# Two-layer graph attention on one core: x and x1 loaded as permuted blocks and transposed on VectorE instead of TensorE

## The chip, the core and the metric

The kernel runs on one core of one Trainium2 chip. A core has five engines that follow their own instruction streams and wait for each other on semaphores: TensorE (matrix products, PE in the profile; its weight loads are PEld), VectorE (DVE), ScalarE (ACT), GpSimd (POOL) and SyncE (SP), which here issues all DMAs. The metric is the device time of one execution in microseconds (us).

## What is computed

The input `x` holds 128 graphs of 64 nodes with 768 features. The first layer is graph attention with 12 heads of 64 features and a gate; the second is masked attention with 6 heads of 128 features. Each layer's result is added to its input and normalized.

```python
# layer 0, per graph
h = einsum('bnd,ade->bane', x, W); th = tanh(h)
attn = th @ w_src + swapaxes(th @ w_dst)          # per head, node by node
attn = softmax(where(adj, leaky(attn), -999))
feat = elu(attn @ h + b)
gate = sigmoid(x @ H_w.T + H_b)
x1 = layernorm(x + gate * feat + (1 - gate) * x)
# layer 1, per graph
q, k, v = x1 @ Wq, x1 @ Wk, x1 @ Wv               # plus biases
out = layernorm(x1 + softmax(mask(q @ k.T / sqrt(128), adj)) @ v @ Wf + bf)
```

## The kernel before

Two graphs make a tile of 128 tokens on the 128 partitions; two tiles make a pair; there are 32 pairs (`NP`). Phase A (to about 1590 us of the profile) runs layer 0 for every pair and the product of layer 1 that gives `v`; phase B runs the rest of layer 1. Only phase A's code changes, apart from the row order in which phase B's weights are loaded.

The large products multiply a pair's two tiles by 768x768 weights with a seven-product scheme for 2x2 blocks. One such product is seven blocks (`Product.matmuls(i)`, i = 0 to 6), each of three matmuls of 128x128 by 128x384; the profile records each matmul twice, so a block is six records (x6) of L203. Blocks read the transposed tiles `T` (blocks 0, 1 and 5) and four sums of parts of them, `S` (blocks 2, 3, 4 and 6), which GpSimd makes in `token_sums` (L252 to L255). After each block, `evict` takes the accumulator out of PSUM: ScalarE copies a `snap` (L381) after blocks 0, 2 and 3, VectorE adds after blocks 1, 4 and 5 (L404 or L423), ScalarE copies after block 6. Block 4 waits for the `snap` of block 2, and block 6 for VectorE's eviction of block 4. Three products run for a pair: h (`start_h`), the gate (`start_g`), and later, on x1, v (`start_v`).

A matmul contracts over partitions, so a tile has to be transposed before it is multiplied. `transposed` (L368) does this on TensorE: six transposes of 128x128 into two PSUM tiles (L375), each copied to SBUF by ScalarE (L376). `chunk0` takes every third column of a half, so that the contraction index runs as (half, partition, c); `chunk1` takes 128 columns in a row. x is transposed with `chunk0`, x1 with `chunk1`, and the rows of the weights are loaded to match.

Nothing is scheduled by a planner. `at(step, f)` files each piece of work under a step; `run` executes the steps in order, and within a step in the order of filing, which goes by pair. This fixes the order of the instructions on every engine, and the order of the DMAs on SP. Pair `p` starts at step `o = 21 p`. In its frame: h blocks at 0 to 6, gate blocks at 7 to 13, v blocks at 56 to 62, so that in a steady window of 21 steps one pair's h and gate blocks are followed by the v blocks of an earlier pair. Around them:

- x of the pair is loaded at -20 (`load`, L314), transposed at -6 and -5, summed at -4.
- For each tile (`Tile0`; tile 1 with s = o, tile 0 with s = o + 5): tanh at s + 6 or 7; the two products with `w_src` and `w_dst` on GpSimd (L444, L451) and their sums on VectorE (L448, L454) at 7 to 9; a small transposition (L456), an exchange through DRAM (`dst_out`, `dst_in`, L462 and L470) and an exchange of halves (`exchange`, L480); adding (L492 on GpSimd, L495 on ScalarE) at 17; mask, maximum, subtraction and exp (L499 to L507) at 18 and 19; sum, reciprocal (L511, L513) and GpSimd's scaling (L514) at 20; the probabilities are transposed on TensorE (L525, L530) at 23 and multiplied by h (L543) at 24; then VectorE's `elu` (L562) and ScalarE's `e` (L569), VectorE's mixes (L573, L574, L582, L583) at 26 and 27, the statistics (L278 to L289) and GpSimd's rstd and shift (L290 to L293) at 28, ScalarE's normalization (L297) at 29, and the store of x1 to DRAM (`spill`, L592) at 30.
- x1 is transposed at 42 and 43 from its SBUF tile and stored transposed for phase B (L663), and summed at 44.

Tiles come from pools with fixed numbers of buffers; an instruction that writes a buffer waits until the last reader of its previous use is done.

Of the kernel before, what the change touches and what calls it, by code (L numbers as in the profile page):

```python
# [9 lines left out]
F32 = mybir.dt.float32  # L10
# [5 lines left out]
P = 128  # L16
# [45 lines left out]
def kernel(  # L62
# [31 lines left out]
    nc = tc.nc  # L94
    NB, S, D = x.shape
# [3 lines left out]
    NC = D // P  # L99
    HALF = D // 2  # L100
    CH = NC // 2
    NT = NB * S // P
    NP = NT // 2
    assert S == 64 and DH == P and E == 64 and HALF == 384 and A == 12

    x_t = x.rearrange("(t g) n d -> t (g n) d", g=2)
# [11 lines left out]
    ident = const.tile([P, P], F32, name="ident")  # L118
# [32 lines left out]
    def load15(wb, src, k):  # L151

        kb, c = divmod(k, 2)
        nc.sync.dma_start(
            wb[:, 3 * kb : 3 * kb + 3, c, :],
            src[k * P : (k + 1) * P, :].rearrange("p (n o) -> p n o", n=3),
        )

    def weight15_sum(wb, k, eng):
        to, a, b, sign = WEIGHT_SUMS[k]  # L160
        eng.tensor_tensor(wb[:, to], wb[:, a], wb[:, b], SIGN[sign])
# [7 lines left out]
    def weight_plain(wb, src, blocks):  # L169
        for kh, oh in blocks:  # L170
                nc.sync.dma_start(
                    wb[:, SLOT[kh, oh]],
                    src[kh * HALF : (kh + 1) * HALF, oh * HALF : (oh + 1) * HALF].rearrange(
                        "(c p) o -> p c o", p=P
                    ),
                )

# [71 lines left out]
    def token_sums(Ss, Ta, Tb):  # L249

        tt = nc.gpsimd.tensor_tensor
        tt(Ss[:, 0], Tb[:, :CH], Tb[:, CH:], ALU.add)  # L252
        tt(Ss[:, 1], Ss[:, 0], Ta[:, :CH], ALU.subtract)
        tt(Ss[:, 2], Ta[:, :CH], Tb[:, :CH], ALU.subtract)
        tt(Ss[:, 3], Ta[:, CH:], Ss[:, 1], ALU.subtract)  # L255
# [14 lines left out]
    x1_d = [spill.tile([P, D], F32, name=f"x1_d{t}") for t in range(NT)]  # L270
    v_d = [spill.tile([P, D], F32, name=f"v_d{t}") for t in range(NT)]
    xT_d = [spill.tile([P, 2, NC, P], F32, name=f"xT_d{p}") for p in range(NP)]
# [27 lines left out]
    def phase_a(ctx):  # L300
        k6 = ctx.enter_context(tc.tile_pool(name="k6", bufs=2))
        k3 = ctx.enter_context(tc.tile_pool(name="k3", bufs=1))
        k1 = ctx.enter_context(tc.tile_pool(name="k1", bufs=1))
        small = ctx.enter_context(tc.tile_pool(name="small", bufs=3))
        psa = ctx.enter_context(tc.tile_pool(name="psa", bufs=4, space=bass.MemoryType.PSUM))

        st = [dict() for _ in range(NP)]
# [6 lines left out]
        def load(p):  # L314
            d = st[p]
            d["x"] = []
            for i in range(2):
                t = xb[:, (2 * p + i) % 7]
                nc.sync.dma_start(t, x_t[2 * p + i])
                d["x"].append(t)  # L320
            d["adj"] = small.tile([P, 2, S], U8, name="adj")
            nc.sync.dma_start(d["adj"], adj_p[p])
# [18 lines left out]

        def load_hrow(oc):

            name = ("gt", "gt", "gt", "z", "e", "th")[oc]
            hrows[oc] = k3.tile([P, D], F32, name=name, bufs=3 if oc < 3 else 1)
            nc.sync.dma_start(hrows[oc], H_w[oc * P : (oc + 1) * P, :])

# [14 lines left out]
        def chunk0(src, k):  # L362
            return src.rearrange("p (h q c) -> p h c q", h=2, c=CH)[:, k // CH, k % CH, :]

        def chunk1(src, k):
            return src[:, k * P : (k + 1) * P]

        def transposed(src, chunk):  # L368

            dst = k3.tile([P, NC, P], F32, name="T", bufs=4)  # L370
            for half in range(2):
                ps = psa.tile([P, CH, P], F32, name="pa")
                for c in range(CH):
                    k = half * CH + c
                    nc.tensor.transpose(ps[:, c, :], chunk(src, k), ident)  # L375
                nc.scalar.copy(dst[:, half * CH : (half + 1) * CH, :], ps)  # L376
            return dst

# [5 lines left out]
        def sums(d):  # L384
            Ss = k6.tile([P, 4, CH, P], F32, name="S")
            token_sums(Ss, *d["T"])
            d["S"] = Ss
# [20 lines left out]
        def start_h(d):  # L408
            d["h"] = [k3.tile([P, D], F32, name="h", bufs=3) for _ in range(2)]
            d["W"] = product(d, lambda i, c: w0_v[:, i, :, c, :], into(d["h"]))  # L410

        def start_g(d):
            d["g"] = [k3.tile([P, D], F32, name="gt", bufs=3) for _ in range(2)]
            d["G"] = product(d, lambda i, c: w1[:, i, c, :], into(d["g"]))

        def start_v(d):
            def sink(k, ps, kept):
                i, half = PLACE[k]
                o = k1.tile([P, HALF], F32, name="v", bufs=3)
                if kept is None:  # L420
                    nc.scalar.copy(o, ps)
                else:
                    nc.vector.tensor_tensor(o, ps, kept, ALU.add)  # L423
                nc.sync.dma_start(v_d[2 * d["p"] + i][:, halves(half)], o)

            d["V"] = product(d, lambda i, c: w2[:, i, c, :], sink)
# [5 lines left out]
        class Tile0:  # L432
# [124 lines left out]
            def elu(self):  # L557

                self.z = k3.tile([P, D], F32, name="z")
                zv = self.z.rearrange("p (j h e) -> p j h e", h=2, e=E)  # L560
                for h2 in range(2):
                    nc.vector.tensor_tensor(  # L562
                        zv[:, :, h2, :],
                        self.pos[h2],
                        b_bc[:, None, :].to_broadcast([P, A // 2, E]),
                        ALU.add,
                    )
                self.e = k3.tile([P, D], F32, name="e")
                nc.scalar.activation(self.e, self.z, AF.Exp, bias=neg_one)  # L569

            def mix1(self):
# [26 lines left out]
        def at(step, *fs):  # L598
            events.setdefault(max(step, 0), []).extend(fs)

        def dense(d, key, i):
            d[key].matmuls(i)
            d[key].evict(i)
# [17 lines left out]
        for p in range(NP):  # L621
            d, o = st[p], N * p
            d["p"] = p
            if p:
                at(max(o - 20, 1), lambda p=p: load(p))

            def xT(d, i):
                d.setdefault("T", []).append(transposed(d["x"][i], chunk0))

            at(o - 6, lambda d=d: xT(d, 0))  # L630
            at(o - 5, lambda d=d: xT(d, 1))
            at(o - 4, lambda d=d: sums(d))
            at(o, lambda d=d: start_h(d))
            at(o + 7, lambda d=d: start_g(d))
            for i in range(7):
                at(o + i, lambda d=d, i=i: dense(d, "W", i))
                at(o + 7 + i, lambda d=d, i=i: dense(d, "G", i))
            for i, s in ((1, o), (0, o + 5)):
                t = Tile0(p, i)
                at(s + 6 + (i == 0), t.tanh, t.cap)  # L640
                at(s + 7, t.src_mul)
                at(s + 8, t.src_sum, t.dst_mul)
                at(s + 9, t.dst_sum, t.dst_out, t.exchange)
                at(s + 13, t.dst_in)
                at(s + 14, t.gate)
                at(s + 17, t.add)
                at(s + 18, t.mask)
                at(s + 19, t.top)
                at(s + 20, t.total)
                at(s + 23, t.probs)  # L650
                at(s + 24, t.aggregate)
                at(s + 25, t.elu)
                at(s + 26, t.mix1)
                at(s + 27, t.mix2)
                at(s + 28, t.norm1)
                at(s + 29, t.norm2)
                at(s + 30, t.spill)

            def x1T(d, i):
                if i == 0:  # L660
                    d["T"] = []
                d["T"].append(transposed(d["x"][i], chunk1))
                nc.sync.dma_start(xT_d[d["p"]][:, i], d["T"][i])  # L663

            at(o + 42, lambda d=d: x1T(d, 0))
            at(o + 43, lambda d=d: x1T(d, 1))

            def reload_T(d):
                d["T"] = []
                for i in range(2):  # L670
                    t = k3.tile([P, NC, P], F32, name="T", bufs=4)
                    nc.sync.dma_start(t, xT_d[d["p"]][:, i])
                    d["T"].append(t)

            if p != NP - 4:
                at(o + 44, lambda d=d: sums(d))

            v = o + {NP - 4: 84, NP - 2: 50, NP - 1: 45}.get(p, 56)
            if p == NP - 4:
                at(v - 7, lambda d=d: reload_T(d))  # L680
                at(v - 3, lambda d=d: sums(d))
            at(v, lambda d=d: start_v(d))
            for i in range(7):
                at(v + i, lambda d=d, i=i: dense(d, "V", i))
# [5 lines left out]
        o = N * (NP - 1)  # L690
# [410 lines left out]
```

## Time and profile before

| | |
|---|---|
| runs (3) | median 3029.0 us, 3027.24 to 3031.79 |
| profiled execution | 3025.7 us, span 3023.9 us |
| TensorE clock granted | 0.993 |
| one pair, steady (start of x's first L375 transposes, 622.25 to 669.72) | 47.47 us |
| TensorE busy, 200 to 1400 us | 199.0 to 199.2 of every 200 us |
| VectorE, ScalarE, GpSimd busy, 600 to 800 us | 132.2, 82.5, 117.3 of 200 us |
| DMA queue of SP | 223,808 packets, 257.16 MB, 25.7% of 16 engines' span |

The profile page gives busy times and groups of instructions. A group is one line of the code on one engine, with count, total and mean duration, and the idle time of the engine just before it, with what ended it. The chain of waits goes back from the last instruction, at each step to what released it. A timeline lists instructions with their start, duration and the idle time before them. Line numbers are those of the kernel before; the sum of the busy times of overlapping matmuls is not their duration.

### The profile page before, as it was taken

What the parts mean: (1) busy time and instruction counts of PE and PEld (TensorE: products, weight loads), DVE (VectorE), ACT (ScalarE), POOL (GpSimd) and SP (SyncE); (2) the same over time, 40 slices, a digit from 0 to 9 for tenths busy, and PEclk for the clock granted to TensorE, in tenths of its full rate; (3) what the DMA queues carried; (4) which work ended last, traced back from release to release, by engine and by line L of the source; (5) the groups of instructions that cost most, each with busy time, mean ns of one, the idle gap of its engine ahead of it and who ended that gap; (6) DMA issues with size and microseconds to landing.
All of it is one profiled execution on the core that took longest, in us unless ns stands there. A gap on an engine that the chain in (4) does not pass through costs nothing.

```text
span 3023.9 us, 49367 instructions
## 1 busy us (share of the span) xinstructions
PE 2935.8 (97%) x18852; PEld 2139.9 (71%) x18852; DVE 1798.6 (59%) x3531; ACT 937.8 (31%) x1743; POOL 1640.8 (54%) x1648
## 2 busy tenths in 40 slices
PE   7899999999999999999899999999999999999997
PEld 4566666666666666666557888888888888888886
DVE  4666666666676666766674555555555555555556
ACT  3343443434434444444422122222112222211221
POOL 3756565665656556565574444554544455454445
PEclk9999999999999999999999999999999999999999
DMA  5232232222322222232252121222112122211221
GB/s 158 67 98 92 89 110 77 98 87 93 105 82 98 82 98 98 84 103 82 87 173 80 49 85 60 78 85 82 57 63 85 59 80 85 81 57 64 85 79 69
DMA packets 224044, 260.31 MB, mean 86 GB/s; under 512 B 91713, under 2 KB 169281, under 8 KB 223809
## 3 DMA queue, kind: packets, MB, share of 16 engines
q1 hardware_dynamic: 223808, 257.16, 25.7%
q8 instruction: 150, 2.46, 0.3%
q14 instruction: 86, 0.70, 0.1%
HBM read 143.43 MB, written 101.06 MB: 81 GB/s over the span
## 4 chain that ended last, share of the span: by engine, by line
PE 66%; POOL 16%; DVE 12%; ACT 2%; issue 2%; DMA 1%; SPq 0%; DVEq 0%; POOLq 0%
PE X L796 29%; PE X L203 29%; POOL S L766 5%; POOL Sc L778 3%; PE pa L375 2%; DVE e L573 2%; POOL xs L754 2%; POOL tmp L444 2%; PE pb L921 2%; PE pb L861 2%; POOL rstd L290 2%; DVE e L574 1%; DVE e L582 1%; DVE st L278 1%; DVE h L404 1%
## 5 line engine op out<-in xcount | busy, mean ns | idle before, releaser
L203 PE MATMUL X<-w,S 128*128 128x384 f32 x2304 | 806.2, 493 | 15.3 <-ACT snap L381 8.3
L796 PE MATMUL X<-S,w 128*128 128x256 f32 x2816 | 669.7, 383 | 18.1 <-ACT q L817 14.8
L203 PEld LDWEIGHTS X<-w,S 128*128 128x128 f32 x2304 | 425.1, 191 | 315.2 <-ACT snap L381 28.1
L203 PE MATMUL X<-w,T 128*128 128x384 f32 x1728 | 608.2, 492 | 1.8 <-ACT T L376 1.0
L796 PEld LDWEIGHTS X<-S,w 128*128 128x128 f32 x2816 | 523.7, 190 | 96.6 <-issue 20.0
L203 PEld LDWEIGHTS X<-w,T 128*128 128x128 f32 x1728 | 320.8, 192 | 201.9 <-issue 4.2
L778 POOL TENSOR_TENSOR Sc<-cT 128x256 f32<-128x256 f32 x224 | 161.4, 730 | 378.6 <-PE X L796 375.0
L796 PE MATMUL X<-w,Sc 128*128 128x256 f32 x1408 | 326.9, 383 | 3.9 <-DVE xs L839 2.6
L839 DVE TENSOR_TENSOR xs<-xs,X 128x256 f32<-128x256 f32 x512 | 208.3, 418 | 179.3 <-PE X L796 147.8
L796 PEld LDWEIGHTS X<-w,Sc 128*128 128x128 f32 x1408 | 263.4, 190 | 47.1 <-DVE xs L839 10.4
L290 POOL TENSOR_TENSOR rstd<-rstd,neg_half 128x1 f32<-128x1 f32 x126 | 69.4, 551 | 398.9 <-DVE rstd L289 398.9
L822 DVE TENSOR_TENSOR k<-k,X 128x256 f32<-128x256 f32 x320 | 133.5, 421 | 218.3 <-PE X L796 168.3
L822 DVE TENSOR_TENSOR q<-q,X 128x256 f32<-128x256 f32 x320 | 131.9, 419 | 203.5 <-PE X L796 122.4
L796 PE MATMUL X<-xb,w 128*128 128x256 f32 x960 | 236.6, 379 | 0.0
L297 ACT ACTIVATE xs<-xs,shift,rstd 128x768 f32<-128x768 f32 x62 | 63.7, 1027 | 471.9 <-POOL shift L293 467.2
L796 PEld LDWEIGHTS X<-xb,w 128*128 128x128 f32 x960 | 181.2, 190 | 24.0
L817 ACT ACTIVATE k<-X,bk_c 128x256 f32<-128x256 f32 x192 | 91.0, 474 | 304.8 <-PE X L796 304.8
L895 POOL TENSOR_TENSOR s<-s,rs 128x384 f32<-128x384 f32 x64 | 53.1, 830 | 243.4 <-DVE rs L894 220.6
L766 POOL TENSOR_TENSOR S<-xb 128x512 f32<-128x512 f32 x104 | 131.6, 1279 | 84.2 <-DMA xb<-xT_d 56.7
L514 POOL TENSOR_TENSOR s<-s,rs 128x768 f32<-128x768 f32 x64 | 94.2, 1472 | 143.9 <-DVE rs L513 134.4
L817 ACT ACTIVATE q<-X,bq_c 128x256 f32<-128x256 f32 x192 | 89.0, 470 | 258.4 <-PE X L796 258.4
L381 ACT COPY snap<-X 128x384 f32<-128x384 f32 x288 | 136.5, 479 | 82.2 <-PE X L203 79.1
(106 smaller groups left out, 4262.8 us busy)
## 6 DMA issues: line engine op xcount, KB each, us to landing
xb<-in_x_dram SPq DMA_DIRECT2D x64, 384.0 KB
s<-dst_d SPq DMA_DIRECT2D x128, 192.0 KB
x_d<-xb SPq DMA_DIRECT2D x64, 384.0 KB
xT_d<-T SPq DMA_DIRECT2D x64, 384.0 KB
v_d<-v SPq DMA_DIRECT2D x128, 192.0 KB
xb<-xT_d SPq DMA_DIRECT2D x32, 768.0 KB
xb<-v_d SPq DMA_DIRECT2D x256, 96.0 KB
xs<-x_d SPq DMA_DIRECT2D x64, 384.0 KB
```

The costliest lines, as they stand in the source:

```text
L203: nc.tensor.matmul(o, self.lhsT(i, c), rhs, start=first and c == 0, stop=last and c == CH - 1, skip_group_check=True,)
L290: nc.gpsimd.tensor_tensor(rstd, rstd, neg_half, ALU.pow)
L297: nc.scalar.activation(r, r, AF.Identity, bias=shift, scale=rstd)
L375: nc.tensor.transpose(ps[:, c, :], chunk(src, k), ident)
L381: nc.scalar.copy(t, ps)
L514: nc.gpsimd.tensor_tensor(self.s, self.s, self.rs[:, :, None].to_broadcast([P, A, S]), ALU.mult)
L766: eng.tensor_tensor(t, group_part(d, r0), group_part(d, r1), op)
L778: nc.gpsimd.tensor_tensor(t, pair_part(d, q, r0), pair_part(d, q, r1), op)
L796: nc.tensor.matmul(ps, self.lhsT(r, slot, c), self.rhs(r, slot, c), start=start and c == 0, stop=stop and c == 1, skip_group_check=True,)
L817: nc.scalar.activation(o[:, b], ps, AF.Identity, bias=bias[:, hd : hd + 1], scale=1.0 if positive else -1.0)
L822: nc.vector.tensor_tensor(o[:, b], o[:, b], ps, ALU.add if positive else ALU.subtract)
L839: nc.vector.tensor_tensor(o, o, ps, ALU.add if positive else ALU.subtract)
```

## The change

x of all pairs but the first, and x1 of all pairs but the last, are no longer transposed on TensorE. Each tile is loaded from DRAM a second time into a buffer `xp` (two buffers) by four DMAs. The DMA with index q fills 32 partitions: partition q*32 + i gets, for each half of the columns and each of four groups t of tokens, 96 consecutive columns of token t*32 + i. With the blocks so placed, VectorE's transposition of 32x32 blocks gives the transposed tile: two instructions of 128x384 for a tile (`turn`). For x the loads are filed at steps -20 and -16 and the transpositions at -6 and -5, as before. x1 is read back from where `spill` put it: loads at 37 (tile 1) and 40 (tile 0), transpositions and the store of the transposed tile at 43 and 46, sums at 47 instead of 44. x of the first pair and x1 of the last stay on TensorE.

x1's transposed columns now have the order of `chunk0`, so Wq, Wk and Wv are loaded with their rows in that order. To make room, `e` shares the buffer of `tmp`, and the pool of small tiles has two buffers instead of three.

```diff
     def load15(wb, src, k):
         kb, c = divmod(k, 2)
+        rows = src[k * P : (k + 1) * P, :] if src is Wf else in_order(src)[k]
         nc.sync.dma_start(
-            wb[:, 3 * kb : 3 * kb + 3, c, :],
-            src[k * P : (k + 1) * P, :].rearrange("p (n o) -> p n o", n=3),
+            wb[:, 3 * kb : 3 * kb + 3, c, :], rows.rearrange("p (n o) -> p n o", n=3)
         )
+    def in_order(src):
+        r = src.rearrange("(h p c) o -> h c p o", h=2, c=CH)
+        return [r[k // CH, k % CH] for k in range(NC)]
...
-                        "(c p) o -> p c o", p=P
+                        "(p c) o -> p c o", p=P
...
-        small = ctx.enter_context(tc.tile_pool(name="small", bufs=3))
+        small = ctx.enter_context(tc.tile_pool(name="small", bufs=2))
...
+        def load_blocks(tile_, src):
+            xp = tile_.rearrange("p (h t r) -> p h t r", h=2, t=4)
+            sv = src.rearrange("(t i) (h q r) -> q i h t r", t=4, h=2, q=4)
+            for q in range(4):
+                nc.sync.dma_start(xp[q * 32 : (q + 1) * 32], sv[q])
+            return xp
+
+        def turn(xp):
+            dst = k3.tile([P, NC, P], F32, name="T", bufs=4)
+            for h in range(2):
+                nc.vector.transpose(
+                    dst[:, h * CH : (h + 1) * CH, :].rearrange("p c (t i) -> p c t i", t=4),
+                    xp[:, h].rearrange("p t (j c) -> p c t j", c=CH),
+                )
+            return dst
+
+        def blocks(src):
+            return load_blocks(k3.tile([P, D], F32, name="xp", bufs=2), src)
...
-                self.e = k3.tile([P, D], F32, name="e")
+                self.e = k3.tile([P, D], F32, name="tmp")
...
+            def xb_in(d, i):
+                d.setdefault("xp", []).append(blocks(x_t[2 * d["p"] + i]))
             def xT(d, i):
-                d.setdefault("T", []).append(transposed(d["x"][i], chunk0))
-            at(o - 6, lambda d=d: xT(d, 0))
-            at(o - 5, lambda d=d: xT(d, 1))
+                d.setdefault("T", []).append(turn(d["xp"][i]))
+            if p:
+                at(o - 20, lambda d=d: xb_in(d, 0))
+                at(o - 16, lambda d=d: xb_in(d, 1))
+                at(o - 6, lambda d=d: xT(d, 0))
+                at(o - 5, lambda d=d: xT(d, 1))
+            else:
+                at(0, lambda d=d: d.update(T=[transposed(t) for t in d["x"]]))
...
-            at(o + 42, lambda d=d: x1T(d, 0))
-            at(o + 43, lambda d=d: x1T(d, 1))
+            def x1_in(d, i):
+                d["xp", i] = blocks(x1_d[2 * d["p"] + i])
+            def x1T(d, i, t):
+                d["x1T", i] = t
+                nc.sync.dma_start(xT_d[d["p"]][:, i], t)
+            if p < NP - 1:
+                at(o + 37, lambda d=d: x1_in(d, 1))
+                at(o + 40, lambda d=d: x1_in(d, 0))
+                at(o + 43, lambda d=d: x1T(d, 1, turn(d["xp", 1])))
+                at(o + 46, lambda d=d: x1T(d, 0, turn(d["xp", 0])))
+            else:
+                for i in range(2):
+                    at(o + 42 + i, lambda d=d, i=i: x1T(d, i, transposed(d["x"][i])))
...
-                at(o + 44, lambda d=d: sums(d))
+                at(o + (47 if p < NP - 1 else 44), lambda d=d: x1_sums(d))
```

More of the change, by code (lines that the diff above doesn't have):

```diff
@@ L342, in load_hrow @@
         def load_hrow(oc):
-            name = ("gt", "gt", "gt", "z", "e", "th")[oc]
+            name = ("gt", "gt", "gt", "z", "tmp", "th")[oc]
             hrows[oc] = k3.tile([P, D], F32, name=name, bufs=3 if oc < 3 else 1)
@@ L363, in chunk0, with transposed @@
             return src.rearrange("p (h q c) -> p h c q", h=2, c=CH)[:, k // CH, k % CH, :]
-        def chunk1(src, k):
-            return src[:, k * P : (k + 1) * P]
-        def transposed(src, chunk):
+        def load_blocks(tile_, src):
[14 more added lines that the diff above has]
+            return load_blocks(k3.tile([P, D], F32, name="xp", bufs=2), src)
+        def transposed(src):
             dst = k3.tile([P, NC, P], F32, name="T", bufs=4)
@@ L373, in transposed @@
                 for c in range(CH):
-                    k = half * CH + c
-                    nc.tensor.transpose(ps[:, c, :], chunk(src, k), ident)
+                    nc.tensor.transpose(ps[:, c, :], chunk0(src, half * CH + c), ident)
                 nc.scalar.copy(dst[:, half * CH : (half + 1) * CH, :], ps)
@@ L657, in phase_a @@
                 at(s + 30, t.spill)
[L659 to L663, printed above, removed]
-            at(o + 42, lambda d=d: x1T(d, 0))
-            at(o + 43, lambda d=d: x1T(d, 1))
+            def x1_in(d, i):
[11 more added lines that the diff above has]
+                    at(o + 42 + i, lambda d=d, i=i: x1T(d, i, transposed(d["x"][i])))
             def reload_T(d):
@@ L673, in reload_T, with x1_sums @@
                     d["T"].append(t)
+            def x1_sums(d):
+                d["T"] = [d["x1T", i] for i in range(2)]
+                sums(d)
             if p != NP - 4:
-                at(o + 44, lambda d=d: sums(d))
+                at(o + (47 if p < NP - 1 else 44), lambda d=d: x1_sums(d))
             v = o + {NP - 4: 84, NP - 2: 50, NP - 1: 45}.get(p, 56)
```

## The prediction

> **What bounds the kernel now.** I read the page's busy times first, then groups by line, the chain of waits over two steady pairs, and VectorE's timeline.
>
> ```profile
> PE 2935.8 (97%) x18852; PEld 2139.9 (71%) x18852; DVE 1798.6 (59%) x3531; ACT 937.8 (31%) x1743; POOL 1640.8 (54%) x1648
> ...
> L375 PE MATMUL pa<-ident,xb 128*128 128x128 f32 x768 | 109.5, 281 | 18.1 <-ACT T L376 12.2 <-DMA xb<-in_x_dram 5.9
> ...
> L456 DVE STREAM_TRANSPOSE sdT<-sd 128x32 f32<-128x32 f32 x64 | 13.5, 212 | 2.2
> ```
>
> In the first line TensorE looks like the only bound; the other two give the duration of what is removed and the only transposition of VectorE before. The chain of waits (start, duration) says otherwise:
>
> ```profile
> 642.09 4.08 PE X L203 x12
> ...
> 646.25 0.56 DVE h L404
> 646.81 1.80 DVE e L573
> ...
> 648.64 0.96 DVE e L574
> 649.60 0.47 DVE h L404
> 650.07 0.88 DVE e L582
> ...
> 650.96 0.96 DVE xb L583
> ...
> 654.59 1.77 POOL tmp L444
> ...
> 656.38 0.95 DVE src L448
> 657.33 0.94 DVE z L562 x2
> ...
> 658.30 0.94 ACT e L569
> 659.23 0.37 ACT snap L381
> ...
> 659.65 4.14 PE X L203 x12
> ...
> 663.81 6.07 PE X L203 x18
> 669.88 0.68 PE pa L375 x6
> ```
>
> Call the blocks of the three products W0-W6 (h), G0-G6 (gate), V0-V6. From eviction of W4 (646.25) to the start of G6 (663.81), 17.56 us, work goes through VectorE, GpSimd and ScalarE; G4 waits for `snap` behind ScalarE's `e`. Only from G6 to W4 is the chain on TensorE. A second route runs beside it:
>
> ```profile
> 677.15 0.56 DVE L423 TENSOR_TENSOR v<-X,snap 128x384 f32<-128x384 f32 x1 [5.53 <-PE X L203]
> 677.63 1.74 DVE L499 TENSOR_TENSOR s<-s,cap 128x768 f32<-128x768 f32 x1
> ...
> 680.73 1.13 DVE L504 TENSOR_TENSOR s<-s,mx 128x768 f32<-128x768 f32 x1
> ...
> 689.91 1.61 DVE L504 TENSOR_TENSOR s<-s,mx 128x768 f32<-128x768 f32 x1
> ...
> 693.73 0.56 DVE L404 TENSOR_TENSOR h<-X,snap 128x384 f32<-128x384 f32 x1
> ```
>
> VectorE idles 5.53 us for V4. Its eviction at 677.15 releases one tile's softmax (mask L499, maximum and subtraction L503 and L504, exp, sum L511, reciprocal L513), then GpSimd's scaling (L514, which ends at 685.59) and its adding for the other tile (L492), ScalarE's L495, and that tile's L499 to L513. Only then, at 693.65, is VectorE free for W4's eviction, which TensorE had ready about 693.7. So both routes have no slack. A pair takes 47.48 us in three legs: 17.56 (W4's eviction to G6's start), 13.34 (G6 at 663.81 to V4's eviction at 677.15) and 16.58 (to W4's eviction at 693.73). The first and third hang on VectorE, GpSimd and ScalarE, the second on TensorE. A leg that grows is paid in every pair; TensorE's work pays only inside the second leg.
>
> [...] L573-L583 take 0.96 us with GpSimd idle, and 1.9 each beside its L161:
>
> ```profile
> 1547.07 2.08 DVE L573 SCALAR_TENSOR_TENSOR e<-e,z 128x768 f32<-128x768 f32 x1
> 1549.18 1.91 DVE L574 SCALAR_TENSOR_TENSOR e<-e,xb 128x768 f32<-128x768 f32 x1
> 1551.12 1.91 DVE L582 SCALAR_TENSOR_TENSOR e<-gt,e 128x768 f32<-128x768 f32 x1
> ```
>
> They alternate: each waits out one GpSimd instruction and then runs some 0.82 us, so in the second L504 above 0.65 of the 1.61 us is such a wait. [...] The trace has only L456, 32 columns in 212 ns. [...] the new loads have 384 B runs. Before, 223,808 packets took 25.7% of 16 engines' 3024 us, 0.056 us each.
>
> **The change, part by part.**
>
> Removed: 124 of 128 groups of six L375 transposes. Each takes 0.65 to 0.68 us of TensorE (669.88 to 670.57): 2.67 us a pair, 82 us in all, with ScalarE's two copies behind each (0.86 us, 107 in all). Of a pair's four groups, the two of x lie between V1 and V4, inside the cycle: -1.36. The two of x1 lie before W0 and W1, beside the second route: 0 once that decides.
>
> Added on VectorE: 248 transpositions of 384 columns. [...] 1.1 a tile (two L278 statistics of the same width take 1.01). Bounds: no extra columns' cost, 0.4 a tile[...]. x's four follow V1's eviction, in the 5.53 us idle before V4's, 4.2 once TensorE's groups are gone: hidden; uncovered they would cost 2.2. x1's first pair follows L513, before W1's eviction, where L499 still waits for L495 (the 2.23 + 1.17 us idle): hidden. x1's second pair stands after the second L504, before L562, L511, L513 and W4's eviction, with no idle time: +1.1. The exp that L511 awaits is already covered by L562.
>
> Moved: GpSimd's four x1 sums (L252-L255), from three steps earlier to behind the second L514. There (639.5 to 644.9) they made the second L504 take 1.61 instead of 0.96: -0.65. Now they begin at the end of L514, while L573 runs. L574, L582 and L583 each meet a sum: one waits about 0.9 us for it, then runs 0.82. L574 ends 0.8 later; W5's eviction, which reads PSUM, intervenes; L582 ends 1.2 later, L583 2.0 later. L289, and behind it GpSimd's L290 and L444, VectorE's L448 and L562, ScalarE's `e`, `snap`, and G4, are all 2.0 later: the 2.30 us idle before G1's eviction is no cover, since L448 already starts as L444 ends. Bounds 0 and 2.5. At 123-126 us, where L574 and L582 met GpSimd's weight sums (1.63 and 1.29 us), TensorE then idled 0.71 us at G4 and 0.81 at G6.
>
> x's sums now follow the second transposition, about 1.9 us before V4's eviction (2.6 before, L252 at 674.56): L499 and L504 then meet L254 and L554 later. L499 waits until +1.10 and ends +1.92; the last sum ends +2.9, L554 +4.6, L504 +5.4 after the eviction instead of +4.71: +0.7 (bounds -0.2, +0.9).
>
> Added on SP: 16 loads a pair, at the 0.38 (L462) to 0.64 us (L480) of small issues: 6 to 10 us, where SP waits some 870 us between 200 and 1400, 34 a pair. x1's loads wait for spills seven and five steps old. The load of tile 1 waits for a transposition of x; behind it are V4's store and L470, which the adding needs 8.5 us after V4's eviction. DMA: 1024 packets a tile, 3.6 us of all engines. I take 0, since every load is issued at least six steps of 2.3 us before its transposition (x1's tile 1 at step 37, turned at 43; tile 0 at 40 and 46); bounds 0 and 1 us a pair. A late load would hold VectorE directly ahead of L562 or W1's eviction.
>
> Nothing: `e` in `tmp`'s buffer (GpSimd's L444 is already behind L290, which is behind L583's end; without that cover up to 1), `small` with two buffers instead of three (the longest life, `adj`'s, is 27 steps, and two buffers allow 42), weights in another row order (same run lengths). At the start SP issues nothing from 19 to 42 us and the DMA share is 0.01 from 30 to 40, so pair 1's loads hide.
>
> **Sum.** First leg 17.56 + 2.0 = 19.56; second 13.34 - 1.36 = 11.98; third 16.58 + 1.1 - 0.65 + 0.7 = 17.73; together 49.27 us, +1.79 a pair. TensorE's own work would need 47.47 - 2.67 = 44.8, so it now waits. x1's transpositions and all three products fall together in about 28 pairs (in the first two and the last two windows something is missing, and there I take no difference): 28 x 1.79 = 50. The profiled run took 3025.7 (span 3023.9 and 1.8 outside): 3076; the median of the runs is 3.3 above it: 3079.
>
> **Rivals.** (1) TensorE stays the bound: 3029 - 82 = 2947. For: 97% busy, VectorE 59%. Against: the chain above, a third of it off TensorE. (2) The other side by one mechanism: x1's sums don't hold up L574-L583[...]. Place: the first leg; price: the 2.0 us. Then -1.36 + 1.1 - 0.65 + 0.7 = -0.2, and with x's sums no worse than before -0.9, times 28 is -25: 3004. It decides where the three are held up less than 0.2 us (with x's sums worse) or 0.9 us (without). For: L583 before was undisturbed. Against: 1547-1555. (3) The transpositions [...] exclude GpSimd too, or a load lands late: +0.8 to +2 more a pair, 3102 to 3135. [...] against: idle SP, loads six steps early.
>
> **Chances.** Forecast 0.66 (own range 3045 to 3110), rival 1 0.08, rival 2 0.12, rival 3 0.12, no change 0.02. The range leaves out rival 1 and the top of rival 3: 2995 to 3125. Under 0.2%, 6 us, a measurement can't tell from no change: faster 0.20, same 0.04, slower 0.76.
>
> **What would show it.** In steady pairs: period 49.3 us; TensorE idle about 2 us before the first L525 transposes (V5, V6, W0, W1 end 7.5 us after V4's eviction, L514 at 5.4 + 2.26 + 1.47 = 9.2) and about 2.4 before G4, behind `snap`; L597, L605 and L606 (the old L574, L582, L583) 1.7, 1.4 and 1.7 us instead of 0.96; [...] the second L504 back to 0.96. A period under 47, or those three near 0.96, makes me wrong; SP waits on DMA, or VectorE waiting for `xp`, would be rival 3.

## The result and the profile after

| | before | after |
|---|---|---|
| runs | median 3028.1 us (3026.9 to 3031.8) | median 3116.6 us (3113.9 to 3118.7) |
| ratio after to before | | 1.029, 95% interval 1.0272 to 1.0307 |
| profiled span | 3023.9 us | 3112.1 us |
| TensorE clock granted | 0.993 | 0.98 |
| one pair, mean of the steady ones, 300 to 1400 us | 47.50 us | 50.40 us |
| W4's eviction to V4's eviction (first and second leg) | 30.92 us | 33.11 us |
| V4's eviction to the next W4's eviction (third leg) | 16.58 us | 17.29 us |

The change makes the kernel 88 us slower. The prediction had 50 us slower. Its direction and the causes that it named held, but two costs were missing from its sum: 3117 lies inside the whole range, 2995 to 3125, and above the forecast's own, 3045 to 3110. After the change the helpers' lines are 5 higher and those from `snap` on 23 higher: L203 is L208, L381 is L404, L404 is L427, L423 is L446, L444 is L467, L448 is L471, L487 (the mask's `cap`) is L510, L499 is L522, L504 is L527, L514 is L537, L525 is L548, L573 to L583 are L596 to L606. The sums L252 to L255 are L257 to L260. The new transposition is L383.

The profile page of the kernel after: busy times, and the shares of the chain that ended last, by engine.

```profile
PE 2894.0 (93%) x18108; PEld 2081.9 (67%) x18108; DVE 2004.0 (64%) x3779; ACT 845.1 (27%) x1495; POOL 1677.9 (54%) x1648
...
PE 46%; DVE 20%; POOL 18%; DMA 6%; SPq 4%; issue 3%; ACT 2%; DVEq 0%; POOLq 0%; ACTq 0%
```

TensorE has 744 matmuls less and a share of 93% instead of 97. Before, it held 66% of the chain and VectorE 12%. DMA's 6% should not be read as late loads: most of it is loads into `xp` that the chain names because they land just as a transposition begins, and VectorE idled for none of them (L383 in the groups below).

VectorE's timeline of the kernel after, for the pair whose W4 is evicted at 677.93 (start, duration, engine, line, instruction, idle time before it and what ended it):

```profile
671.84 0.96 DVE L522 TENSOR_TENSOR s<-s,cap 128x768 f32<-128x768 f32 x1 [2.28 <-ACT s L518]
...
673.82 0.96 DVE L527 TENSOR_TENSOR s<-s,mx 128x768 f32<-128x768 f32 x1
674.70 1.30 DVE L383 STREAM_TRANSPOSE T<-xp 128x384 f32<-128x384 f32 x2
...
677.93 0.52 DVE L427 TENSOR_TENSOR h<-X,snap 128x384 f32<-128x384 f32 x1
678.37 2.07 DVE L596 SCALAR_TENSOR_TENSOR tmp<-tmp,z 128x768 f32<-128x768 f32 x1
680.48 1.64 DVE L597 SCALAR_TENSOR_TENSOR tmp<-tmp,xb 128x768 f32<-128x768 f32 x1
...
682.51 1.28 DVE L605 SCALAR_TENSOR_TENSOR tmp<-gt,tmp 128x768 f32<-128x768 f32 x1
683.83 1.64 DVE L606 SCALAR_TENSOR_TENSOR xb<-xb,tmp 128x768 f32<-128x768 f32 x1
685.39 1.02 DVE L510 TENSOR_SCALAR cap<-adj 128x128 f32<-128x128 uint8 x1
...
690.73 0.95 DVE L471 TENSOR_REDUCE src<-tmp 128x12 f32<-128x768 f32 x1 [2.47 <-POOL tmp L467]
```

GpSimd's timeline of the same stretch:

```profile
678.16 1.47 POOL L537 TENSOR_TENSOR s<-s,rs 128x768 f32<-128x768 f32 x1 [7.23 <-DVE rs L536]
679.59 1.72 POOL L257 TENSOR_TENSOR S<-T 128x384 f32<-128x384 f32 x1
681.38 1.60 POOL L258 TENSOR_TENSOR S<-S,T 128x384 f32<-128x384 f32 x1
682.94 1.71 POOL L259 TENSOR_TENSOR S<-T 128x384 f32<-128x384 f32 x1
684.62 1.71 POOL L260 TENSOR_TENSOR S<-T,S 128x384 f32<-128x384 f32 x1
...
688.88 1.81 POOL L467 TENSOR_TENSOR tmp<-th,ws_bc 128x768 f32<-128x768 f32 x1
```

Read the two side by side. L597, L605 and L606 each begin while a sum runs and end 0.8 us after it (L257 ends at 681.31, L597 at 682.12): 1.64, 1.28 and 1.64 us where 0.96, 0.95 and 0.96 stood before. L596 does the same with the scaling L537, as it did before. L510 ends just after the fourth sum: 1.02 us, where the timeline of before has 0.22. The second L527 is back at 0.96, and the second pair of transpositions of x1 stands right behind it, 1.30 us for two.

TensorE's timeline of the kernel after, the same pair:

```profile
669.56 0.87 PE L548 MATMUL pa<-ident,s 128*128 128x128 f32 x6 [1.80 <-POOL s L537]
...
686.82 4.03 PE L208 MATMUL X<-w,S 128*128 128x384 f32 x12
694.06 3.59 PE L208 MATMUL X<-w,S 128*128 128x384 f32 x6 [3.21 <-ACT snap L404]
697.44 2.45 PE L208 MATMUL X<-w,T 128*128 128x384 f32 x6
699.73 2.10 PE L208 MATMUL X<-w,S 128*128 128x384 f32 x6
```

It waits 3.21 us for `snap` before G4 (694.06). And then something is in no part of the prediction: G4, six records of work that take 2.0 us elsewhere, takes until 697.44, 3.4 us. Such a block is called slow from here on. Groups by line and shape, 300 to 1400 us (count, sum, mean ns, idle time before). Before:

```profile
L203 PE MATMUL X<-w,S 128*128 128x384 f32 x1663 | 577.8, 490 | 4.9 <-ACT snap L381 4.1
L487 DVE TENSOR_SCALAR cap<-adj 128x128 f32<-128x128 uint8 x23 | 5.0, 219 | 0.0
```

and after:

```profile
L208 PE MATMUL X<-w,S 128*128 128x384 f32 x1574 | 562.0, 504 | 67.9 <-ACT snap L404 67.9
L383 DVE STREAM_TRANSPOSE T<-xp 128x384 f32<-128x384 f32 x176 | 112.0, 690 | 0.0
L548 PE MATMUL pa<-ident,s 128*128 128x128 f32 x264 | 38.4, 283 | 24.9 <-POOL s L537 24.9
L510 DVE TENSOR_SCALAR cap<-adj 128x128 f32<-128x128 uint8 x22 | 22.3, 1015 | 0.0
```

Over 22 pairs TensorE idles 67.9 / 22 = 3.1 us before G4 and 24.9 / 22 = 1.1 us before the first probabilities. The transposition takes 0.69 us, and VectorE never idled for one, so no load was late.

### The profile page after: what moved, and what is told of

Its sections match the earlier page's. It is cut to its first block, busy times and chain, and to the rows that moved or that the text cites. A ratio compares the mean times of both kernels' runs of the same rounds, so it can differ in the third digit from the quotient of the medians.

```text
span 3112.1 us, 48544 instructions
## 1 busy us (share of the span) xinstructions
PE 2894.0 (93%) x18108; PEld 2081.9 (67%) x18108; DVE 2004.0 (64%) x3779; ACT 845.1 (27%) x1495; POOL 1677.9 (54%) x1648
## 2 busy tenths in 40 slices
DMA packets 358954, 309.04 MB, mean 99 GB/s; under 512 B 226624, under 2 KB 304192, under 8 KB 358720
## 3 DMA queue, kind: packets, MB, share of 16 engines
q1 hardware_dynamic: 358720, 305.95, 31.9%
## 4 chain that ended last, share of the span: by engine, by line
PE 46%; DVE 20%; POOL 18%; DMA 6%; SPq 4%; issue 3%; ACT 2%; DVEq 0%; POOLq 0%; ACTq 0%
PE X L838 28%; PE X L208 14%; POOL S L808 5%; POOL Sc L820 3%; DVE T L383 2%; POOL tmp L467 2%; DMA xp<-in_x_dram 2%; DVE tmp L596 2%; DMA xp<-x_d 2%; DVE tmp L597 2%; POOL xs L796 2%; DVE z L585 2%; PE pb L963 2%; POOL rstd L295 2%; DVE xb L606 2%
## 5 line engine op out<-in xcount | busy, mean ns | idle before, releaser
L208 PE MATMUL X<-w,S 128*128 128x384 f32 x2304 | 827.8, 506 | 99.1 <-ACT snap L404 94.5
L208 PEld LDWEIGHTS X<-w,S 128*128 128x128 f32 x2304 | 442.4, 196 | 415.7 <-ACT snap L404 114.3
L208 PE MATMUL X<-w,T 128*128 128x384 f32 x1728 | 614.3, 499 | 15.3 <-DVE T L383 13.3
L208 PEld LDWEIGHTS X<-w,T 128*128 128x128 f32 x1728 | 333.9, 196 | 243.9 <-issue 43.3
L537 POOL TENSOR_TENSOR s<-s,rs 128x768 f32<-128x768 f32 x64 | 94.2, 1471 | 316.3 <-DVE rs L536 313.2
L404 ACT COPY snap<-X 128x384 f32<-128x384 f32 x288 | 133.8, 475 | 118.1 <-PE X L208 117.8
```

Source lines behind the costliest of these rows:

```text
L208: nc.tensor.matmul(o, self.lhsT(i, c), rhs, start=first and c == 0, stop=last and c == CH - 1, skip_group_check=True,)
L404: nc.scalar.copy(t, ps)
L537: nc.gpsimd.tensor_tensor(self.s, self.s, self.rs[:, :, None].to_broadcast([P, A, S]), ALU.mult)
```

## The experiments

Theory A: the legs that the prediction's chain runs through VectorE, ScalarE and GpSimd count as fully as TensorE's own; x's part shortens the second, x1's part lengthens the first (GpSimd's sums beside VectorE's mixes) and the third (the second pair of transpositions). Rivals: the loads cost; VectorE's transpositions cost wherever they stand; TensorE bounds. Each run was timed beside the kernel before on the same chip. Period and legs are read from VectorE's timeline between 300 and 1400 us (starts of L510, of W4's and of V4's eviction), as means over 20 to 24 pairs.

| run | us | ratio to before, 95% interval | period | legs 1 and 2 | leg 3 |
|---|---|---|---|---|---|
| before | 3028 | | 47.50 | 30.92 | 16.58 |
| predicted for the change | 3079 | | 49.27 | 31.54 | 17.73 |
| the change | 3117 | 1.0272 to 1.0307 | 50.40 | 33.11 | 17.29 |
| loads only | 3028 | 0.9992 to 1.0010 | 47.48 | 30.85 | 16.63 |
| x only | 3014 | 0.9936 to 0.9970 | 47.06 | 29.68 | 17.38 |
| x1 only | 3145 | 1.0366 to 1.0397 | 51.54 | 35.03 | 16.50 |
| turn early | 3077 | 1.0145 to 1.0175 | 49.15 | 32.22 | 16.97 |
| turn and sums early | 3022 | 0.9970 to 0.9986 | 47.20 | 29.69 | 17.51 |
| filler | 3111 | 1.0258 to 1.0289 | 50.27 | 33.09 | 17.18 |
| more filler | 3105 | 1.0243 to 1.0274 | 50.07 | 32.19 | 17.87 |
| x only, first turn early | 2987 | 0.9850 to 0.9880 | 46.00 | 29.39 | 16.61 |
| all early | 2985 | 0.9842 to 0.9871 | 46.01 | 29.69 | 16.32 |
| adding early | 2981 | 0.9826 to 0.9859 | 45.59 | 29.35 | 16.23 |
| probabilities later | 2980 | 0.9826 to 0.9859 | 45.56 | 29.71 | 15.85 |

**The loads alone.**

```diff
-    at(o - 6, lambda d=d: xT(d, 0))
-    at(o - 5, lambda d=d: xT(d, 1))
+    at(o - 6, lambda d=d: d.update(T=[transposed(d["x"][0])]))
+    at(o - 5, lambda d=d: d["T"].append(transposed(d["x"][1])))
-    at(o + 43, lambda d=d: x1T(d, 1, turn(d["xp", 1])))
-    at(o + 46, lambda d=d: x1T(d, 0, turn(d["xp", 0])))
+    for i in range(2):
+        at(o + 42 + i, lambda d=d, i=i: x1T(d, i, transposed(d["x"][i])))
-    at(o + (47 if p < NP - 1 else 44), lambda d=d: x1_sums(d))
+    at(o + 44, lambda d=d: x1_sums(d))
```

> All transpositions back on TensorE, and x1's sums at step 44; the loads into xp stay, every one of them, and nobody reads them. The weights' row order, e in tmp's buffer and the two buffers of small stay too. Theory A (the loads, the row order and the buffers cost nothing, as predicted): 3029 us as before, within 6. Rival (queue and DMA work of the loads, or a tighter buffer, is part of the loss): 3040 to 3110.

Measured: 3028 us, the same within 0.1%. Its queue carries what the changed kernel's carries, 358,720 packets and 305.95 MB. So the loads, the weights' row order, `e` in `tmp`'s buffer and the two buffers of `small` cost nothing together as long as no instruction reads the loaded tiles: the rival falls. In the changed kernel none waited for them either, so all of the loss lies in where the transpositions and the sums stand.

**x alone, and x1 alone.** For x alone:

```diff
-    at(o + 37, lambda d=d: x1_in(d, 1))
-    at(o + 40, lambda d=d: x1_in(d, 0))
-    at(o + 43, lambda d=d: x1T(d, 1, turn(d["xp", 1])))
-    at(o + 46, lambda d=d: x1T(d, 0, turn(d["xp", 0])))
+    for i in range(2):
+        at(o + 42 + i, lambda d=d, i=i: x1T(d, i, transposed(d["x"][i])))
-    at(o + (47 if p < NP - 1 else 44), lambda d=d: x1_sums(d))
+    at(o + 44, lambda d=d: x1_sums(d))
```

> Only x by blocks and transposed on VectorE; x1 transposed on TensorE at steps 42 and 43 and its sums at step 44, as before. Theory A (the period is the sum of three legs, and what x1's part puts into the legs off TensorE is the loss): first leg 17.56 as before, second 11.9 as in the changed kernel, third 16.6 to 16.8, so about 46.3 us a pair, -1.2 against before: 2990 to 3005 us. Rival (the loads by 384-byte runs on SP and the DMA queues cost, x's as much as x1's): half of the loss, about 3070. Rival (TensorE alone bounds): 3029 less x's half of the removed 82 us, about 2985 to 2990.

For x1 alone:

```diff
-    at(o - 20, lambda d=d: xb_in(d, 0))
-    at(o - 16, lambda d=d: xb_in(d, 1))
-    at(o - 6, lambda d=d: xT(d, 0))
-    at(o - 5, lambda d=d: xT(d, 1))
+    at(o - 6, lambda d=d: d.update(T=[transposed(d["x"][0])]))
+    at(o - 5, lambda d=d: d["T"].append(transposed(d["x"][1])))
```

> Only x1 by blocks and transposed on VectorE, its sums at step 47; x on TensorE as before. Theory A: the first leg as in the changed kernel (+2.7 before block G4, +1.5 behind it), the second leg 13.3 as before, the third about +0.5: 3.4 to 4.9 us a pair more than before, 3123 to 3165 us, slower than the changed kernel (3117). Rival (each block-loaded tile costs alike): half of the loss, about 3070. Rival (TensorE bounds): about 2990.

Measured: 3014 and 3145 us. The two halves go opposite ways, as theory A has it and the rivals don't; x1's half alone is even slower than the whole change: x's groups are still in its second leg, and G4 is slow in all of its 21 pairs. But x alone gained 14 us, about half of what was expected. Legs 1 and 2 are right (29.68: 17.69 and 11.98 in the pair at 640), and leg 3 has 17.38 instead of 16.6 to 16.8. Groups of VectorE in that run, 300 to 1400 us:

```profile
L527 DVE TENSOR_TENSOR s<-s,mx 128x768 f32<-128x768 f32 x47 | 86.3, 1837 | 1.6
```

Before, the same line (L504) had a mean of 1.364 us. The prediction's term for x's sums, +0.7 in leg 3, is in this run in full (+0.80), and I had written it down to about nothing because the changed kernel shows only a little of it.

**The two places of x1's work.** Two single edits, one on top of the other: x1's tile 0 turned three steps earlier, and then the sums moved back to where they were.

```diff
-                at(o + 46, lambda d=d: x1T(d, 0, turn(d["xp", 0])))
+                at(o + 43, lambda d=d: x1T(d, 0, turn(d["xp", 0])))
```

> The changed kernel with x1's tile 0 turned at step 43, right behind tile 1, where VectorE idles; the sums stay at step 47. Theory A: the transposition pair of 1.3 us leaves the third leg, the first stays long: 1.3 us a pair less than in the changed kernel at most, 3075 to 3095 us. Rival (the transpositions cost wherever VectorE does them, or the loads do): 3117 as before the edit, within 10.

```diff
-                at(o + (47 if p < NP - 1 else 44), lambda d=d: x1_sums(d))
+                at(o + 44, lambda d=d: x1_sums(d))
```

> As the run with x1's tile 0 turned at step 43, and x1's sums at step 44 as in the kernel before, so that GpSimd does them ahead of the second scaling and not beside the mixes. Theory A: the first leg is back at 17.5, the second stays 11.9, the third as before: 1.1 to 1.4 us a pair less than before, 2988 to 3000 us, faster than both kernels; the three mixes take 0.96 us again and the cap 0.22. Rival (loads, queue or transpositions themselves cost): 3070 or more.

Measured: 3077 and 3022 us. The 31 tiles (62 transpositions) that the first edit moves cost 40 us less in VectorE's idle time than behind the second L527, some of it through fewer slow blocks (below): the rival that transpositions cost anywhere falls. Of the 1.25 us a pair, only 0.32 come out of leg 3, where W4's eviction then waits about 0.5 us for TensorE. Most of the rest comes out of the first leg, where the scaling L537 begins earlier and L596 takes 1.44 instead of 2.07 us beside it. Moving four GpSimd instructions a pair back by three steps takes off another 55 us. In the second run the groups of VectorE, 300 to 1400 us, read:

```profile
L383 DVE STREAM_TRANSPOSE T<-xp 128x384 f32<-128x384 f32 x188 | 118.8, 687 | 7.1 <-DMA xp<-x_d 6.8
L527 DVE TENSOR_TENSOR s<-s,mx 128x768 f32<-128x768 f32 x47 | 86.1, 1832 | 1.6
...
L597 DVE SCALAR_TENSOR_TENSOR tmp<-tmp,xb 128x768 f32<-128x768 f32 x47 | 45.0, 958 | 1.6
...
L510 DVE TENSOR_SCALAR cap<-adj 128x128 f32<-128x128 uint8 x23 | 5.0, 219 | 0.0
```

L597 and L510 are where they were before the change. That is the first leg's loss, undone by its cause. The total missed the forecast of 2988 to 3000 by the same L527 as above, and by 7 us of loads that now come late in some pairs.

**x's sums.** The transposition of x's first tile is moved into VectorE's 2.5 us wait for GpSimd ahead of the second L471, so that the sums start about 1 us sooner:

```diff
-                at(o - 6, lambda d=d: xT(d, 0))
+                at(o - 9, lambda d=d: xT(d, 0))
```

once on top of x alone, once on top of turn and sums early (there x1's loads are also filed at 35 and 38 instead of 37 and 40).

> As the run with only x by blocks (3014 us), with the transposition of x's first tile at step -9 instead of -6: it then falls into VectorE's 2.5 us wait for GpSimd ahead of L471, and x's sums start behind L515, 1.0 us sooner. Theory A (the 0.87 us that the third leg had more than before in that run is the predicted meeting of x's sums with L522 and L527): third leg 16.6 again, 0.8 us a pair less, about 2990 us (2985 to 3000); L527's mean 1.8 falls to about 1.35. Rival (the 0.87 comes from elsewhere): 3014 within 6.

> As the run with x1's tile 0 turned at step 43 and sums at 44 (3022 us), with x's first tile turned at step -9, and x1's loads at steps 35 and 38 instead of 37 and 40, since tile 0's came late in some pairs (VectorE waited 7 us for it between 300 and 1400). Theory A: 0.8 us a pair from x's sums and 0.2 from the load: 2988 to 3000 us, the same as with x alone, since x1's transposes on TensorE lay off the path. Rival (TensorE has become the bound once the legs are short): lower than with x alone by up to 30, 2960 to 2975. Rival (VectorE is too full): 3015 or more.

Measured: 2987 and 2985 us. Leg 3 is at 16.61 and 16.32, and L527 in the first of them:

```profile
L527 DVE TENSOR_TENSOR s<-s,mx 128x768 f32<-128x768 f32 x48 | 65.7, 1369 | 1.7
```

So the excess was x's sums. The second run lies just under the forecast of its first theory, 2988 to 3000. The two runs are within 0.1% of each other, though the second has 62 tiles' transposes fewer on TensorE. In the first TensorE has nothing to wait for any more (1.8 us idle before its L208 in 1100 us): there it is the bound, at 46.00 us. In the second TensorE idles 0.45 us before G4 and 0.75 before L548 in each pair, and the legs are the bound, by chance at nearly the same length.

**What TensorE's saving is worth then.** With all early as the base, tile 0's adding (L515) and the DMA ahead of it are filed so that GpSimd adds before tile 1's scaling and not behind it; then tile 1's probabilities are filed one step later on TensorE.

```diff
-                at(s + 13, t.dst_in)
+                at(s + (13 if i else 11), t.dst_in)
-                at(s + 17, t.add)
+                at(s + (17 if i else 14), t.add)
```

> As the run with every piece early (2985 us), and tile 0's adding for the attention (L515) at its step 14 instead of 17, its input's DMA (L493) at 11 instead of 13: GpSimd then adds ahead of the first tile's scaling L537 and not behind it, so that L518 and tile 0's mask L522 no longer wait for that scaling. Theory A (with TensorE's own work at 44.8 us a pair, the two legs off TensorE still hold the period at 46.0): the third leg shrinks by about 1.1 us (L522's idle time behind W1's eviction), TensorE's idle 1.2 us a pair goes, period 44.8 to 45.0, 2950 to 2958 us. Rival (TensorE or something else bounds at 46.0 already): 2985 within 5. Rival (L515 now meets L527, and the DMA comes too late): 2990 or more.

```diff
-                at(s + 23, t.probs)
-                at(s + 24, t.aggregate)
+                at(s + 23 + i, t.probs)
+                at(s + 24 + i, t.aggregate)
```

> As the run with tile 0's adding early (2981 us, period 45.59), with tile 1's probabilities transposed on TensorE one step later (behind block W2) and multiplied one step later: TensorE then no longer idles 0.75 us for the scaling L537. Theory A (those 0.75 us are all that lies above TensorE's own 44.8): period 44.85, 2956 to 2964 us. Rival (the later product delays the first leg by as much): 2981 within 6.

Measured: 2981 and 2980 us, both short of the forecasts and both where a rival had put them (2985 within 5, 2981 within 6). TensorE's timeline of the first:

```profile
667.49 0.87 PE L548 MATMUL pa<-ident,s 128*128 128x128 f32 x6 [0.75 <-POOL s L537]
```

and of the second:

```profile
669.75 2.17 PE L208 MATMUL X<-w,S 128*128 128x384 f32 x6 [0.17 <-ACT snap L404]
...
691.41 2.20 PE L208 MATMUL X<-w,S 128*128 128x384 f32 x6 [0.57 <-ACT snap L404]
```

The wait before G4 is gone in the first, but that before L548 is not: it follows V4's eviction through tile 1's softmax, which the edit didn't shorten. 45.59 - 0.75 = 44.84 us is TensorE's own work, the 44.8 of the prediction, so the period there is not TensorE's alone. In the second the 0.75 reappear as 0.17 + 0.57 before W2 and G4: the rival of that run was right. What would remove them was not tried. These two are still the fastest versions here, 1.6% under the kernel before.

**The slow block.** Work that nobody needs is put between G3 and G4, so that TensorE idles less while G4 still waits for `snap`. The diff is that of the larger filler; the smaller one does `CH` (three) transposes and is filed twice.

```diff
+        def filler(d):
+            ps = psa.tile([P, CH, P], F32, name="pa")
+            for k in range(8 * CH):
+                nc.tensor.transpose(ps[:, k % CH, :], chunk0(d["x"][0], k % CH), ident)
...
+            at(o + 10, lambda d=d: filler(d))
```

> The changed kernel with two groups of six TensorE transposes, whose result nobody uses, between the gate's blocks G3 and G4, so that 1.3 of the 3.2 us that TensorE idles before G4 are filled; G4 itself still waits for snap. Theory A (after more than 3 us of idleness the next block is slow, 3.4 instead of 1.94 us): idle time before G4 about 1.9 us, G4 back at 2.0 us, 1.0 to 1.5 us a pair less, 3074 to 3090 us. Rival (the slow block has another cause, or the lost time is taken up by another wait): 3117 or more.

> The changed kernel with 24 TensorE transposes, whose result nobody uses, between blocks G3 and G4. The earlier run with a filler had only six of them (two groups of three, 0.65 us), and left TensorE idle for 2.5 us and slow in 13 of 22 pairs. These 24 take 2.6 of the 3.2 us. Theory A (idle time of 2.3 us or more before G4 slows TensorE down in about two of three pairs, at 1.4 us each): no slow blocks, 0.8 to 1.1 us a pair less than in the changed kernel, 3083 to 3097 us. Rival (the slow blocks cost nothing in the end, since another wait takes their place): 3111 or more.

The first of these texts says two groups of six; the kernel that ran had two groups of three, half of it. Measured: 3111 and 3105 us. Read from G4's start to V4's eviction, which takes 16.1 us in a pair without a slow block, G4 was slow in 14 of 22 pairs in the changed kernel (idle 3.2 us before G4 in 20 of them, 1.8 in two), in 14 of 22 with the small filler (2.54 us), in 10 of 22 with the turn early (about 2.3 us), and in none of 22 with the large filler (0.5 us); a slow pair takes about 1.4 us more. TensorE's timeline with the large filler (L405):

```profile
687.63 2.89 PE L405 MATMUL pa<-ident,xb 128*128 128x128 f32 x24
691.01 2.20 PE L208 MATMUL X<-w,S 128*128 128x384 f32 x6 [0.49 <-ACT snap L409]
693.05 2.10 PE L208 MATMUL X<-w,T 128*128 128x384 f32 x6
```

G4 takes 2.04 us and no G4 is slow any more: idleness causes the slow blocks.

The traces also record the clock granted to TensorE, and it tells why the same idle time is followed by a slow block in some pairs only. In the changed kernel, between 300 and 1400 us, it falls to 0.50 for 3.41 us at a time (once for twice that), and these stretches begin whole multiples of 3.41 us apart (442.14, 493.34, 544.54, 619.63, 694.72 us), as they do in the kernel before (98.83, 112.49, 1477.82 us). Two pairs on this grid (window, its length, busy time of TensorE, of its weight loads, VectorE, ScalarE and GpSimd, then PEclk, the granted clock, and the DMA's share and rate), the first with a slow G4 from 694.06 on, the second with a G4 of 2.04 us from 392.38 on:

```profile
691.31:694.72 3.41, 0.66 (x2) 0.49 (x3) 3.34 (x7) 2.02 (x4) 1.26 (x1) 1.00 0.16 62
694.72:698.13 3.41, 3.41 (x7) 1.74 (x6) 3.21 (x4) 0.41 (x1) 0.00 (x0) 0.50 0.24 57
...
387.53:390.94 3.41, 1.64 (x6) 0.63 (x4) 1.89 (x4) 0.78 (x1) 3.29 (x2) 1.00 0.29 115
390.94:394.36 3.42, 1.99 (x6) 1.25 (x7) 3.32 (x5) 2.42 (x4) 0.00 (x0) 1.00 0.02 2
394.36:397.77 3.41, 3.41 (x11) 1.82 (x10) 3.31 (x8) 0.00 (x0) 0.00 (x0) 1.00 0.50 135
```

Both waits last 3.2 us. The first puts 2.75 us of idleness into one window, and the next window runs at half the clock; the second is split into 1.77 and 1.43 us, and nothing happens. In the trace of the changed kernel, between 300 and 1400 us and with the ends of matmuls as the profile models them, each of the 16 windows at full clock in which TensorE idled 1.98 us or more was followed by one at half the clock, and none of the 287 with 1.86 us or less was. In that of the kernel before no window of this stretch had more than 0.39 us of idleness, and the clock stayed full. The filler's transposes count as work here: with the large filler the mean clock granted in the profiled execution was 0.992, against 0.98 in the changed kernel and with the small filler.

With the slow blocks gone, legs 1 and 2 lose 33.11 - 32.19 = 0.92 us a pair, but leg 3 grows from 17.29 to 17.87, so that only 12 of the forecast 20 to 34 us are gained. Each theory had half of it. Leg 3 grows because V4 now comes earlier against x's sums: the prediction's +0.7, which the slow blocks had covered up. The first filler missed its forecast because I had taken 3 us of idleness as the point where the slowness begins, from the idle times of 1.8, 2.1 and 3.2 us that I had seen; its 2.54 us could still put 1.98 into one window.

## Why the prediction was right, and where its sum was short

**The bound.** Right: TensorE sets only the second of the three legs. That the legs add up to the period holds by their definition; what shows the bound is that two edits which left TensorE's work as it was, and moved only transpositions and sums on VectorE and GpSimd, brought 3117 down to 3022. TensorE's own 44.8 us a pair was never reached. The rival "TensorE stays the bound" would have needed 2947.

**x's groups, -1.36 in the second leg.** Right: G6 at 699.73 to V4's eviction at 711.61 is 11.88 us, against 11.98.

**x1's groups, worth nothing.** Right while the legs are the longer: with x's part alone the kernel takes 3014 us, and with x1's groups gone from TensorE too (turn and sums early) 3022, no less. They are worth 6 us where TensorE is the bound with them (2987) and the legs are shortened without them (2981).

**Loads, queues, buffers: 0.** Right (3028). In the changed kernel no transposition waited for a load.

**The second transposition, +1.1.** Mis-sized: 0.69 us each, hence +1.3. The 1.1 was my estimate, which nothing in the trace of before shows: the two L278 beside it, at 1.01, are another operation. Moving it gained 1.25 us a pair, about 0.25 of that from fewer slow blocks (an estimate: 4 of 22 pairs at 1.4 us). 690 ns (L383) against 211 (L479) for 352 more columns is 1.36 ns a column; whether strided reading has a part in it no run here shows. The rival that it excludes GpSimd too falls: the four of x ran in 2.48 us from 655.85 on with GpSimd's L577 and L515 beside them.

**x1's sums, +2.0 in the first leg.** Right in where the time goes (each of the three ends 0.8 us after the sum that it met), and too small. From W4's eviction to the end of L606 is 7.54 us, where the pair at 693.73 before has 5.67: +1.9, as worked out. But the step counted three meetings and there are four: the fourth sum ends behind L606, and L510, which the prediction never named, waits for it (0.22 to 1.02 us, +0.80). I had looked for operations with two inputs in SBUF; L510 has one. The trace shows it all the same: L510 alone takes 0.22 us, and 1.02 beside L260, which ends at 686.33, 0.08 us before it. The reduction L471 takes 0.95 us beside GpSimd's L474.

**TensorE idles before G4.** Predicted at 2.4 us, measured 3.2, and priced at the wait alone. The missing term is that the block behind it is slow: +0.92 us a pair. The trace shows half the clock (PEclk 0.50; G4 takes up to 4.0 us, at 340.91, instead of 2.04) for 3.41 us at a time. Its windows don't move with the pairs: of 20 waits of 3.2 us before G4, 14 were followed by a slow block and six were not. And a window need not be idle throughout: 1.98 us were enough.

**TensorE idles before the first probabilities.** Predicted at about 2 us (its terms, 5.4 + 2.26 + 1.47, give 9.13 and not 9.2, and so 1.6), measured at 1.1 as a mean. In two of the 22 pairs it was this wait that filled a window, and the half clock fell on the blocks behind it (from 619.63 us on) and not on G4.

**x's sums, +0.7 in the third leg.** Right where TensorE is not slow (+0.80 with x alone; leg 3 of 17.87 with the large filler, predicted 17.73). In the changed kernel the slow blocks make V4 late in most pairs, so part of it is hidden: leg 3 is 17.29.

**The second L504, -0.65.** Right: 0.96.

**The sum.** Legs 1 and 2: +0.64 predicted, +2.19 measured; the missing terms, 0.80 and 0.92, are a little more than the difference, since the sums' own part was 1.9 and not 2.0. Leg 3: +1.15 predicted, +0.71 measured. Per pair 1.79 (from a period of 47.48) became 2.90. And 28 pairs were too few: 88 us are about 30 times 2.90. That the whole range held 3117 owes something to luck: it reached so far for rival 3, and what rival 3 named (a transposition that excludes GpSimd, a late load) was not the cause; of its +0.8 to +2 us a pair, only the transposition's excess of 0.2 came true.

## What to carry to other kernels

Work taken off a 97% busy engine is worth only what it shortens of the chain; here one of two equal halves was worth 14 us and the other cost 116, and both only because of where the replacing work stood. When work is moved beside another engine, list every instruction that runs in the new window on both engines, to the end of the last one moved, single-input ones too. A wait put before TensorE can cost more than its own length: here it did when 1.98 us or more of idleness fell into one 3.41 us window of the granted clock. Waits of 1.8 us before G4, and waits of 3.2 us filled down to 0.5 with work that nobody needs, did not.

## What was not expected of the hardware

- VectorE's single-input TENSOR_SCALAR (128x128, uint8 to f32) was held up by GpSimd's two-input operation: 0.22 us alone, 1.02 beside it. The transposition of 32x32 blocks (four in 2.48 us) and the reduction (0.95 us) were not.
- VectorE's transposition of 128x384 f32 with strided reading took 0.69 us, that of 128x32 took 0.21.
- The clock granted to TensorE changed only on a grid of 3.41 us, in the traces of the kernel before and of the changed one. In the second, between 300 and 1400 us, a full-clock window with 1.98 us or more of idleness was followed by one at half the clock in 16 of 16 cases, one with 1.86 us or less in none of 287; a block of 2.04 us then took up to 4.0. f32 transposes on TensorE, put into the wait, kept the clock up: 0.992 with 24 of them, 0.98 without.
